# A GpSimd memset in front of every third indirect DMA of the edge scores

## The chip, the cores and the metric

The kernel runs on one core of one Trainium2 chip. The metric is the device time of one execution in microseconds (us), lower is better. PE is the matrix engine, DVE the vector engine, ACT the scalar engine, POOL is GpSimd, SP the engine that issues most of the plain DMAs. A name with a small q (POOLq, SPq) is the sequencer of that engine.

## The reference

Two graph layers are applied to `x` (16 batches, 1024 nodes, 256 features) with one adjacency matrix `adj` (1024 x 1024), most of whose entries are zero. The second layer is the part that matters here:

```python
pre_u = einsum('bud,dk->buk', h_t, W1[:d])
pre_v = einsum('bvd,dk->bvk', h_t, W1[d:])
hidden = relu(pre_u[:, :, None, :] + pre_v[:, None, :, :] + b1)
S = sigmoid(einsum('buvk,ko->buvo', hidden, W2)[..., 0] + b2[0])
a_t = einsum('buv,bud->bvd', S * A_a, h_t)
m_t = einsum('uv,bud->bvd', A_m, h_t) * h_t
z_t = beta1*h_t + beta2*(einsum(a_t, Wa) + ba) + beta3*(einsum(m_t, Wm) + bm)
```

Here `A_a` and `A_m` are both `adj`, and `h_t` is the output of the first layer (a softmax attention over `adj`, all 1024 x 1024 entries). `S` is needed only where `adj` is not zero, because it is multiplied by `A_a`. The kernel therefore computes the scores `S` edge by edge, not for all pairs.

## The kernel before, in words

The first layer and the node projections run batch by batch, on PE above all. For each batch the kernel leaves in DRAM the projections of both ends (`pu_d`, `pw_d`), the features multiplied by `Wa` (`ha_d`) and a partial output (`zb_d`). The batches form three groups of 5, 5 and 6 (`GROUPS`), and a row of `pu_d` or `pw_d` holds one node for all batches of the group.

The edges were sorted before into 21 tiles of 128 lists. A tile has up to 8 places per list, so that there are 135 slots (`SLOTS`), each with 128 edges, one per partition. For each group and each slot `k` the scores go as follows:

- `fetch` (L1201) has POOL issue an indirect DMA that gathers 128 rows of `pw_d` into a buffer `gv` (L1212), and, on the first slot of each tile, one that gathers `gu` out of `pu_d` (L1205). There are five `gv` buffers (`GV`), and slot `k + 3` is fetched when slot `k` is begun (`AHEAD`).
- `compare` (L1235) has DVE combine `gv` with `gu`, in two halves (L1241).
- `sums` (L1248) has ACT add up the columns of each batch into `lg` (L1255); on some slots of the last group DVE does it (L1252). This frees the `gv` buffer.
- `gates` applies the tanh to a part of some 16 slots (L1263), DVE adds 1 (L1282), and the part's scatters are put on the list `late`.
- `scatter` (L1219) has POOL issue an indirect DMA that writes 128 scores of a slot into the dense matrix `sa_d` (L1221). `first`, inside `scores`, takes one or two from `late` after each fetch; what is left after the last slot is issued in one go.

When a group's scores are in `sa_d`, SP loads blocks of it as `sat` (L1325), ACT turns them into `apart` (L1338), DVE multiplies by `adj` (L1343) and PE makes the products with `ha_g` (`gather`, L1356). SP must not load a block before all scatters of the group have landed.

The scores of one group run beside the first layer of the next group's batches, beside the messages (`pm`, L1151), and those of the third group beside the final products (L1356) of the first two. What each engine does next is written out by hand: every step is given a planned time in a `Timetable`, and the steps are emitted in the order of those times. Nothing is reordered at run time; an engine that waits holds up all that stands behind it in its own order.

`upper` (L525) is a 128 x 128 constant in SBUF. PE reads it in four matmuls and weight loads at the start (L563, L768), the last of them 71.6 us into the span, and nothing reads it later.

Of the kernel before, what the change touches and what calls it, by code (L numbers as in the profile page):

```python
# [371 lines left out]
def edge_layers(  # L372
# [36 lines left out]
    nc = tc.nc  # L409
# [115 lines left out]
    upper = const.tile([P, P], F32, name="upper")  # L525
# [383 lines left out]
    st = {}  # L909
# [288 lines left out]
    SA = 7  # L1198
    late = []

    def fetch(g, k):  # L1201
        t, s = SLOTS[k]
        if s == 0:
            gu = st["gu", t] = pools["gath", g].tile([P, SIZE[g] * R], F32, name="gu", bufs=2)
            nc.gpsimd.indirect_dma_start(  # L1205
                out=gu,
                out_offset=None,
                in_=pu_d[g],
                in_offset=bass.IndirectOffsetOnAxis(ap=key_u[:, t : t + 1], axis=0),
            )  # L1210
        gv = st["gv", k] = pools["gath", g].tile([P, SIZE[g] * R], F32, name="gv", bufs=GV)
        nc.gpsimd.indirect_dma_start(  # L1212
            out=gv,
            out_offset=None,
            in_=pw_d[g],
            in_offset=bass.IndirectOffsetOnAxis(ap=idx_v[:, t, s : s + 1], axis=0),
        )

    def scatter(g, lg, i, k):  # L1219
        t, s = SLOTS[k]  # L1220
        dma = nc.gpsimd.indirect_dma_start(  # L1221
            out=sa_d[g],
            out_offset=bass.IndirectOffsetOnAxis(ap=idx_s[:, t, s : s + 1], axis=0),
            in_=lg[:, i, : SIZE[g]],
            in_offset=None,
            bounds_check=N * N - 1,
            oob_is_err=False,
        )
        tc.declare_no_dep(dma.ins, group=f"sa{g}", reason="edges of their own")
        tc.add_to_no_dep_group(f"sa{g}", dma.ins)  # L1230
# [34 lines left out]
    def scores(g, start, end, on_vector):  # L1265

        for k in range(len(SLOTS)):
            time = start + k * (end - start) / len(SLOTS)

            def first(k=k):  # L1270
                for n in range(AHEAD) if k == 0 else ():
                    fetch(g, n)
                if k + AHEAD < len(SLOTS):
                    fetch(g, k + AHEAD)
                for _ in range(min(len(late), 2 if len(late) > PARTS[0] - 4 else 1)):
                    late.pop(0)()

            def last(k=k):
                k0, k1 = place_of(k)
                lg = st["lg", k0]  # L1280
                part = lg[:, : k1 - k0, : SIZE[g]]
                nc.vector.tensor_scalar(part, part, 1.0, None, ALU.add)  # L1282
                late.extend(lambda i=i: scatter(g, lg, i, k0 + i) for i in range(k1 - k0))
# [441 lines left out]
@with_exitstack  # L1725
def tile_graph_layers(ctx: ExitStack, tc: tile.TileContext, *args):
    nc = tc.nc
    I32 = mybir.dt.int32
    hold = ctx.enter_context(tc.tile_pool(name="hold", bufs=1))
    flag = hold.tile([1, 1], I32, name="flag")  # L1730
    edge_layers(tc, *args, flag)
    over = nc.values_load(
        flag[0:1, 0:1],
        min_val=0,
        max_val=1,
        skip_runtime_bounds_check_because="it is a comparison's result",
    )
    with tc.If(over > 0):
        dense_layers(tc, *args)
# [43 lines left out]
```

## Time and profile before

| | us |
|---|---|
| median of 10 runs | 2094.79 |
| lowest and highest of them | 2089.59, 2097.35 |
| the profiled execution | 2090.47 |
| its span, first to last instruction | 2088.8 |

The profiled execution is 1.67 us longer than its span, and 4.32 us below the median of the runs. The granted clock of PE was 0.995 in it. Busy shares of the span were: PE 97%, DVE 75%, ACT 66%, POOL 54%. The 16 DMA engines moved 644.37 MB, 308 GB/s over the span; the queue of the POOL DMAs had 47.6% of the engines' time.

In a line of instruction groups, the figures after the bar are the busy time in us, the mean of one in ns, and the idle time of the engine just before them with what ended most of it. "issue" means that the engine waited for nothing that the profile shows.

### The profile page before, as it was taken

How to read it: one execution, taken by the hardware profiler on the slowest of the kernel's cores; microseconds unless marked ns; L12 is line 12 of the kernel's file. 1: busy time of each engine (PE TensorE's matmuls, PEld its weight loads, DVE VectorE, ACT ScalarE, POOL GpSimd, SP SyncE). 2: the span in 40 equal slices, each digit the busy share in tenths (PEclk: the TensorE clock that was granted, in tenths of full speed). 3: DMA queues.
4: the chain of work that ended last, by engine and by line, in shares of the span. 5: the costliest groups of instructions: out<-in, count | busy, mean ns of one | idle time of the engine just before them, and what ended most of it. 6: DMA issues, size and time to landing. Idle time of an engine off the chain costs nothing.

```text
span 2088.8 us, 28949 instructions
## 1 busy us (share of the span) xinstructions
PE 2025.0 (97%) x8566; PEld 1550.8 (74%) x8566; DVE 1567.1 (75%) x2348; ACT 1374.1 (66%) x4842; POOL 1136.6 (54%) x986
## 2 busy tenths in 40 slices
PE   7999999999999999999999999899999989999998
PEld 5887888777777768576888886456667666778887
DVE  6798886577777677678878885578888878885544
ACT  4212222386867778587888886567888879886654
POOL 2122221257676777668777776666777757673000
PEclk9999999999999999999999999999999999999999
DMA  6597777778888888789999998899999999997873
GB/s 218 209 340 293 290 294 268 245 251 297 282 280 287 271 289 276 263 302 294 304 310 340 311 321 307 316 384 415 386 398 368 411 416 400 391 403 272 282 234 122
DMA packets 248023, 644.37 MB, mean 308 GB/s; under 512 B 37170, under 2 KB 137522, under 8 KB 245810
## 3 DMA queue, kind: packets, MB, share of 16 engines
q0 software_dynamic: 82528, 349.79, 47.6%
q1 hardware_dynamic: 129506, 258.44, 33.6%
q10 hardware_dynamic: 35824, 34.22, 4.7%
q8 instruction: 69, 1.13, 0.2%
q14 instruction: 96, 0.79, 0.1%
HBM read 479.56 MB, written 162.92 MB: 308 GB/s over the span
## 4 chain that ended last, share of the span: by engine, by line
PE 53%; DVE 15%; DMA 14%; ACT 9%; issue 6%; POOL 3%; ACTq 0%; SPq 0%; DVEq 0%; POOLq 0%
PE pv L1053 17%; PE pm L1151 9%; PE pp L1091 7%; DVE gv L1241 6%; DMA gv<-pw_d,idx_v 6%; PE pzg L1356 5%; ACT gv L1255 5%; PE pf L999 4%; DMA sat<-sa_d 3%; PE pea L1119 3%; ACT apart L1338 3%; PE pzh L1356 2%; PE pz L1171 2%; DVE eT L1040 2%; DMA ha_g<-ha_d 2%
## 5 line engine op out<-in xcount | busy, mean ns | idle before, releaser
L1255 ACT ACTIVATE gv<-gv 128x272 f32<-128x272 f32 x2058 | 856.1, 419 | 304.5 <-DVE gv L1241 204.1
L1241 DVE TENSOR_TENSOR gv<-gv,gu 128x680 f32<-128x680 f32 (+1 forms) x810 | 704.4, 906 | 104.5 <-DMA gv<-pw_d,idx_v 100.9
L1212 POOL DMA_INDIRECT gv<-pw_d,idx_v x405 | 486.8, 1202 | 315.3 <-ACT gv L1255 188.7
L1221 POOL DMA_INDIRECT sa_d<-lg,idx_s x405 | 503.1, 1242 | 129.3 <-issue 104.5
L1053 PE MATMUL pv<-feats,eT 128*128 128x257 f32 x2048 | 471.1, 381 | 7.2 <-DVE eT L1040 6.4
L1151 PE MATMUL pm<-adj_sb,xh 128*128 128x512 f32 x1024 | 454.0, 597 | 2.9 <-DVE xh L1067 2.9
L1053 PEld LDWEIGHTS pv<-feats,eT 128*128 128x128 f32 x2048 | 381.3, 190 | 73.2 <-DVE eT L1040 16.8
L1255 ACT ACTIVATION_READ_ACCUMULATOR gv<-gv 128x1 f32 x2058 | 389.1, 189 | 0.0
L1356 PE MATMUL pzg<-ha_g,apart 128*128 128x256 f32 x1536 | 366.7, 381 | 19.6 <-DVE apart L1343 18.9
L1151 PEld LDWEIGHTS pm<-adj_sb,xh 128*128 128x128 f32 x1024 | 194.7, 192 | 223.5 <-issue 220.7
L1356 PEld LDWEIGHTS pzg<-ha_g,apart 128*128 128x128 f32 x1536 | 288.6, 190 | 79.7 <-DVE apart L1343 32.1
L1338 ACT COPY apart<-sat 128x640 f32<-128x640 f32 (+1 forms) x192 | 264.6, 1392 | 80.3 <-PE pzh L1356 45.5
L1343 DVE TENSOR_TENSOR apart<-apart,adj_sb 128x640 f32<-128x640 f32 (+1 forms) x192 | 165.9, 866 | 128.0 <-ACT apart L1338 127.7
L1091 PE MATMUL pp<-wuv,hT 128*128 128x272 f32 x1024 | 249.4, 393 | 4.5 <-ACT end L1105 3.8
L1091 PEld LDWEIGHTS pp<-wuv,hT 128*128 128x128 f32 x1024 | 193.8, 190 | 51.6 <-issue 6.7
L1040 DVE SCALAR_TENSOR_TENSOR eT<-row,col,grown 128x512 f32<-128x512 f32 x256 | 182.8, 744 | 30.7 <-ACT col L986 30.1
L845 POOL DMA_INDIRECT table_d<-rec,at x52 | 57.4, 1104 | 259.6 <-DVE rec L838 157.6
L1084 ACT COPY hT<-ph 128x512 f32<-128x512 f32 x96 | 55.2, 576 | 114.0 <-PE ph L1073 113.9
L1119 PE MATMUL pea<-wa,hT 128*128 128x256 f32 x512 | 121.0, 379 | 0.0
L1171 PE MATMUL pz<-wm,mT 128*128 128x256 f32 x512 | 116.0, 379 | 0.6 <-DVE mT L1162 0.6
L999 PE MATMUL pf<-w1T,xT 128*128 128x257 f32 x512 | 114.9, 381 | 0.5 <-DVE xT L957 0.5
L1356 PE MATMUL pzh<-ha_g,apart 128*128 128x256 f32 x384 | 114.2, 379 | 0.0
(184 smaller groups left out, 1590.3 us busy)
## 6 DMA issues: line engine op xcount, KB each, us to landing
sa_d<-zero SPq DMA_DIRECT2D x128, 512.0 KB, 5.9
sat<-sa_d SPq DMA_DIRECT2D x128, 320.0 KB, 8.8
sat<-sa_d SPq DMA_DIRECT2D x64, 384.0 KB, 5.6
pu_d<-end SPq DMA_DIRECT2D x64, 272.0 KB, 4.3
pw_d<-end SPq DMA_DIRECT2D x64, 272.0 KB, 5.8
ha_d<-ea SPq DMA_DIRECT2D x64, 256.0 KB, 5.1
zb_d<-zb ACTq DMA_DIRECT2D x64, 256.0 KB, 7.8
xh<-in_x_dram SPq DMA_DIRECT2D x15, 1024.0 KB, 12.3
```

Of the source, the lines that this page charges most:

```text
L999: nc.tensor.matmul(pfs[i], lhsT=st["xT"][:, h, c * P : (c + 1) * P], rhs=w1T[:, h, :], start=(h == 0), stop=(h == H - 1),)
L1040: nc.vector.scalar_tensor_tensor(st["eT", b, k, n][:, i, :], st["row"][:, cols], st["col"][:, j : j + 1], grown[:, j, cols], ALU.max, ALU. ...
L1053: nc.tensor.matmul(pv[:, : D + 1], lhsT=st["eT", b, k, j // 4][:, j % 4, i * P : (i + 1) * P], rhs=st["feats", b][:, j, :], start=(j == 0) ...
L1091: nc.tensor.matmul(pp[:, k, :R], lhsT=st["hTi", b, i][:, h, k * P : (k + 1) * P], rhs=wuv[:, side, h, :], start=(h == 0), stop=(h == H - 1),)
L1119: nc.tensor.matmul(pp[:, k, :], lhsT=st["hTi", b, i][:, h, k * P : (k + 1) * P], rhs=wa[:, h, :], start=(h == 0), stop=(h == H - 1),)
L1151: nc.tensor.matmul(pm, lhsT=held[b][:, c, h * P : (h + 1) * P], rhs=adj_sb[:, c, span], start=(c == 0), stop=(c == C - 1),)
L1212: nc.gpsimd.indirect_dma_start(out=gv, out_offset=None, in_=pw_d[g], in_offset=bass.IndirectOffsetOnAxis(ap=idx_v[:, t, s : s + 1], axis=0),)
L1221: dma = nc.gpsimd.indirect_dma_start(out=sa_d[g], out_offset=bass.IndirectOffsetOnAxis(ap=idx_s[:, t, s : s + 1], axis=0), in_=lg[:, i, : ...
L1241: nc.vector.tensor_tensor(mv, mv, mu, op)
L1255: nc.scalar.activation(one[:, j, :], one[:, j, :], AF.Copy, accum_out=lg[:, i, j : j + 1])
L1338: nc.scalar.copy(apart.rearrange("p g v -> p v g"), sat)
L1356: nc.tensor.matmul(st["pzg", g, vc][j // 4][:, j % 4, :], lhsT=apart[:, j, :], rhs=ha, start=(c == 0 and j % 2 == 0), stop=(c == C - 1 and ...
```

## The change

`fetch` and `scatter` call a new function in front of each indirect DMA. It counts the calls, and on every third it has POOL write zeros over `upper`. The count `st["issued"]` runs on through the slots and groups. The indirect DMAs that build the edge lists at the start (L845) don't call it.

```diff
+    def breathe():
+
+        st["issued"] = st.get("issued", 0) + 1
+        if st["issued"] % 3 == 0:
+            nc.gpsimd.memset(upper, 0.0)
+
     def fetch(g, k):
         t, s = SLOTS[k]
         if s == 0:
+            breathe()
             gu = st["gu", t] = pools["gath", g].tile([P, SIZE[g] * R], F32, name="gu", bufs=2)
             nc.gpsimd.indirect_dma_start(
...
+        breathe()
         gv = st["gv", k] = pools["gath", g].tile([P, SIZE[g] * R], F32, name="gv", bufs=GV)
         nc.gpsimd.indirect_dma_start(
...
     def scatter(g, lg, i, k):
         t, s = SLOTS[k]
+        breathe()
         dma = nc.gpsimd.indirect_dma_start(
```

## The prediction

> **What bounds the kernel now.** I read the page's busy shares first, then its chain of waits, then the costliest groups, and after that POOL's own order of instructions. The shares:
>
> ```profile
> PE 2025.0 (97%) x8566; PEld 1550.8 (74%) x8566; DVE 1567.1 (75%) x2348; ACT 1374.1 (66%) x4842; POOL 1136.6 (54%) x986
> ```
>
> PE leaves 64 us of 2088.8 idle. POOL, the engine that the change loads, looks half free. That is the first thing to distrust: the share leaves out what lies between POOL's instructions, and it averages over stages without scores. The chain that ended last and the two large POOL groups:
>
> ```profile
> PE 53%; DVE 15%; DMA 14%; ACT 9%; issue 6%; POOL 3%; ACTq 0%; SPq 0%; DVEq 0%; POOLq 0%
> L1212 POOL DMA_INDIRECT gv<-pw_d,idx_v x405 | 486.8, 1202 | 315.3 <-ACT gv L1255 188.7
> L1221 POOL DMA_INDIRECT sa_d<-lg,idx_s x405 | 503.1, 1242 | 129.3 <-issue 104.5
> ```
>
> Only half of the chain is PE; the rest is the scores' loop (gather, compare, sum) and the loads behind it. The scatters have 104.5 us of idle time before them, over 343 of them, that nothing released: 0.30 us each. POOL's order of instructions shows the same 0.30 us between any two indirect DMAs that stand back to back. So an indirect DMA occupies POOL for its length and 0.30 us more. The scores of group 1 are 135 slots in the 460 us from 856 to 1316, which is 3.41 us a slot. A slot needs one gather (1.202), one scatter (1.242) and 63/405 of a `gu` gather (1.182): 2.63 us, and 2.156 gaps of 0.30 bring it to 3.27. POOL is thus 96% taken there, not 54%. The busy time of POOL in stretches of 50 us (busy, number of instructions, clock, DMA share, GB/s):
>
> ```profile
> 800.00:850.00 50.00, 39.52 (x30) 1.00 0.86 279
> 950.00:1000.00 50.00, 39.64 (x35) 1.00 0.94 303
> 1150.00:1200.00 50.00, 38.88 (x31) 1.00 0.92 312
> 1400.00:1450.00 50.00, 31.67 (x24) 1.00 1.03 413
> ```
>
> With 0.30 us for each instruction, 1.5 us of the first stretch are free, none of the second, 1.8 of the third, 11.1 of the last. Summed over the 29 stretches from 450 to 1900 it is 160 us free of 1450. And the chain itself goes through POOL in places; here is a piece of it (start, length, what):
>
> ```profile
> 1313.99 0.95 POOL gv L1212
> 1314.94 0.30 issue
> 1315.24 1.01 POOL sa_d L1221
> 1316.25 0.30 issue
> 1316.56 0.21 POOL gu L1205
> ```
>
> **The change, part by part.** Nothing is removed, no data moves, and no transfer is added. 63 + 405 + 405 = 873 indirect DMAs call the counter, so 291 memsets are added, all on POOL, spread evenly between 369 and 1904 us. Ten fall in a stretch of 30 DMAs.
>
> *One memset.* The trace has three of this shape at its start, two of them here by form, and the start times of those around:
>
> ```profile
> L537 POOL MEMSET ones<- 128x128 f32 x1 | 0.2, 201 | 0.0
> L526 POOL MEMSET upper<- 128x128 f32 x1 | 0.2, 194 | 0.0
> 1.34 0.19 POOL L526 MEMSET upper<- 128x128 f32 x1
> 1.61 0.29 POOL L527 TENSOR_SCALAR_AFFINE_SELECT upper<-upper 128x128 f32<-128x128 f32 x1
> 1.85 0.20 POOL L537 MEMSET ones<- 128x128 f32 x1
> 1.99 0.95 POOL L659 MEMSET zero<- 128x1024 f32 x1
> ```
>
> So 0.20 us by its length, and by the starts 0.27 (with a successor that reads what it wrote) or 0.14 us (with one that does not). None stands between two indirect DMAs. Bounds for that: nothing, if the memset runs inside the 0.30 us gap that is there anyway; 0.50 us, if it is followed by a gap of its own, 0.20 + 0.30. At the start a plain POOL DMA followed an iota with no such gap (iota 2.90 + 0.37, DMA at 3.23), so I take 0.20. The page "Perfetto Trace Analysis" of the Trainium skill, section "GPSIMD Engine Instruction", says that the reported length of a POOL instruction is unreliable, and that the spacing of starts should be used. By that rule the price is the 0.14 above, and each sum below is seven tenths of what I give.
>
> *What it waits for.* The write over `upper` needs PE's last read of it, at 71.6 us: no wait by 369 us. The memset is emitted in front of the wait of its DMA for a free buffer. Where POOL waits for ACT to free `gv` (188.7 us, 130 gathers) the memset falls into that wait and costs nothing; the cover is gone where the DMA stands under "issue". Behind the memset stand its DMA and all later ones; DVE's compare waits for a gather, and a group's first `sat` load for its last scatter.
>
> *VectorE.* The page "SBUF — State Buffer", section "SBUF: two separate sides", says that GpSimd and VectorE share one pair of ports, held for a whole instruction, against a VectorE operation in a two-port mode, or with two SBUF inputs if the GpSimd one reads. That speaks against the change only for the first kind, since a memset reads nothing. The compares (two SBUF inputs) took 849/860/1079 ns (least, median, longest) beside POOL's DMAs. I charge nothing; were each memset to hold up DVE for its 0.20 us, it would be 58 us of DVE time, spread over all stages.
>
> *What lies on the path.* I counted in the chain the POOL DMAs that follow one another without another engine between, and the gather that ends each such run:
>
> - 451 to 463: 8; 848 to 850: 2; 864 to 869: 4; 894: 1
> - 1035 to 1059: 15; 1188 to 1191: 3; 1303 to 1334: 23; 1372: 1; 1387 to 1388: 2
> - 1436 to 1459: 5; 1585 to 1595: 5; 1847 to 1853: 5
> - the scatters that are left after the last slot, 1876.83 to 1904.85: 18
>
> The last run counts whole although the chain names ACT in the middle of it, since its gaps are the same 0.30 us, and PE does wait at its end:
>
> ```profile
> 1902.60 0.97 POOL L1221 DMA_INDIRECT sa_d<-lg,idx_s  x1 [0.30 <-ACT apart L1338]
> 1903.88 0.97 POOL L1221 DMA_INDIRECT sa_d<-lg,idx_s  x1 [0.30 <-issue]
> 1932.78 1.99 PE L1356 MATMUL pzg<-ha_g,apart 128*128 128x256 f32 x8 [0.56 <-DVE apart L1343]
> 1936.01 1.99 PE L1356 MATMUL pzg<-ha_g,apart 128*128 128x256 f32 x8 [0.38 <-DVE apart L1343]
> ```
>
> After 1936 PE runs without a wait to the end, so what the scatters lose is lost. Together 92 DMAs, some 31 memsets, at 0.20 us 6.1 us (0 to 15.3 by the bounds).
>
> *Off the path.* Elsewhere the free time per stretch covers ten memsets (2.0 us), but for four: 800 (short by 0.5), 950 (2.5), 1100 and 1150 (0.25 each). Those at 800 and 1150 lie beside counted runs; I add the 2.5 of 950, where the chain is now all PE and would turn to the gathers. Three slots of lead, some 10 us, are no cover for that: the gather issued at 463.00 took the chain 12.19 us to land, and DVE waits 100.9 us for gathers in 45 places as it is.
>
> Sum: 6.1 + 2.5 = 8.6 us. On the profiled execution's 2090.47 that gives 2099.1; the median of the runs lies 4.3 higher, and the prediction is 2094.8 + 8.6 = 2103.4 us.
>
> **The rivals.**
>
> *POOL becomes the bound of the scores.* At 0.50 us a memset, a slot of group 1 would need 3.27 + 0.36 = 3.63 us against the 3.41 that it has. The shortfall of all stretches, each against its own free time, sums to 28 us; with 15.3 on the path that is 43 us, 2138. For: the constant gap of 0.30, whose cause the trace does not show. Against: the gapless instructions at the start.
>
> *Covered altogether.* The memset runs in the gap or in waits, price 0 to 0.14: at most 4.3 on the path, 2095 to 2099. For: the sequencer has free time, and the gap is the same whatever came before. That the memset is not executed at all, as a write that nobody reads, I leave out: the copy into `warm` at L503 is never read either, and it is in the trace.
>
> *Faster.* From 1350 to 1850 the DMA share is 1.0, and the chain goes through landings of gathers (5.6% of the span, 117 us) and of `sat` (3.5%, 73 us). POOL's DMAs have a least length of 0.93 to 0.97 us and means of 1.20 and 1.24, so that some 220 us of them are hold-ups. If a pause lets earlier descriptors drain, the next DMA is shorter by what it waited, and the transfers collide less. With a tenth off both landings, 19 us, the net is 8.6 - 19 = -10, 2084. It decides from where landings shorten by over 4.5% of 190 us. Against: POOL issues in bursts because it is behind, and what is issued later lands later.
>
> **How the numbers follow.** Forecast 0.44, POOL as the bound 0.20, covered 0.14, faster 0.22. A difference of 0.2% is 4.2 us, about what a measurement of this kernel can tell from none. The first two end slower, 0.64; covered is the same, 0.14; faster 0.22. The likeliest case alone spans 2099 (0.14 us and nothing off the path) to 2110 (chain at its upper bound). Of the range, 2084 takes in the faster case as priced and 2138 the bound case; I leave out some 0.1 on either side.
>
> **What would show it.** 291 memsets of about 0.20 us on POOL, its busy time up by 58 us; gaps of 0.30 us in front of DMAs after a memset too (none for "covered", two of them for the bound). The last scatter, relative to the last gather, later by 18/3 x 0.20 = 1.2 us. More "DVE gv from DMA gv" than 100.9 us, and PE's idle time up by the sum. It is wrong if the mean lengths of L1212 and L1221 fall by over 0.1 us, or if the chain no longer touches POOL in the places named.

## The result, and the profile after

The changed kernel takes 2098.64 us (median of 14 runs, 2095.37 to 2103.26). The kernel before, measured beside it again, takes 2092.13 us over 50 runs. The ratio is 1.0032 with a 95% interval of 1.0023 to 1.0040: the change costs 6.5 us (4.8 to 8.4). The profiled execution of the changed kernel took 2099.09 us, its span 2097.4 against 2088.8 before.

The added lines move the later lines of the kernel by 7 (the `gu` gather), by 8 (the `gv` gather) and by 9 (from the scatter on). So L1212, L1221, L1241, L1255 and L1356 of before are now L1220, L1230, L1250, L1264 and L1365. From the page of the changed kernel, the shares and the two large POOL groups:

```profile
PE 2028.5 (97%) x8566; PEld 1551.9 (74%) x8566; DVE 1568.0 (75%) x2348; ACT 1374.9 (66%) x4842; POOL 1188.4 (57%) x1277
L1220 POOL DMA_INDIRECT gv<-pw_d,idx_v x405 | 481.6, 1189 | 292.5 <-ACT gv L1264 188.0
L1230 POOL DMA_INDIRECT sa_d<-lg,idx_s x405 | 497.2, 1228 | 114.0 <-issue 93.5
```

POOL has 291 instructions more and is busy for 52 us more. DVE's and ACT's busy times are within 1 us of those before. PE's idle time went from 64 to 69 us, and its busy time from 2025.0 to 2028.5, at a mean granted clock of 0.994 instead of 0.995. The memsets themselves, by form, with busy time and mean ns:

```profile
L1205 POOL MEMSET upper<- 128x128 f32 x291 | 67.8, 233 | 0.0
```

Each takes 0.233 us. What one adds to POOL's order is another matter, and POOL's instructions in order show it (start, length; in brackets the idle time before, and what ended it):

```profile
951.01 1.01 POOL L1230 DMA_INDIRECT sa_d<-lg,idx_s  x1 [0.30 <-issue]
951.99 0.25 POOL L1205 MEMSET upper<- 128x128 f32 x1
952.41 1.24 POOL L1220 DMA_INDIRECT gv<-pw_d,idx_v  x1 [0.16 <-issue]
953.95 1.01 POOL L1230 DMA_INDIRECT sa_d<-lg,idx_s  x1 [0.30 <-issue]
```

The scatter ends at 952.02 and the next gather starts at 952.41: 0.39 us between them, where two DMAs without a memset have 0.30 (953.65 to 953.95). The memset starts just before the DMA ends, and the gap behind it shrinks to 0.16. So it adds 0.09 us, not 0.23: most of it lies in time that POOL lost anyway between two indirect DMAs. This is no single case: at the 231 places of the profile where a memset stands between two indirect DMAs and the second waited for nothing else, the distance is 0.37 to 0.40 us. At most 291 x 0.09 = 26 us were added to POOL's order (a memset that falls into a wait adds nothing), against some 160 us that were free, and yet 6.5 us arrived at the end.

Where they arrived is seen in two long stretches (busy time and number of instructions of PE, PEld, DVE, ACT and POOL, then clock, DMA share, GB/s). The first stretch holds the scores of group 0, the second those of group 1. The kernel before:

```profile
385.00:856.00 471.00, 470.35 (x1937) 349.71 (x1936) 351.36 (x561) 347.81 (x1460) 314.45 (x265) 1.00 0.84 274
856.00:1316.00 460.00, 449.76 (x1965) 352.48 (x1964) 354.63 (x583) 356.96 (x1493) 334.10 (x286) 0.99 0.90 306
```

The changed kernel:

```profile
385.00:856.00 471.00, 471.00 (x1940) 350.57 (x1940) 352.38 (x561) 348.57 (x1464) 330.07 (x354) 1.00 0.85 275
856.00:1316.00 460.00, 445.31 (x1951) 350.44 (x1950) 354.56 (x582) 355.04 (x1480) 345.06 (x376) 0.99 0.89 302
```

In the first PE is as far as before (1940 matmuls against 1937). In the second it does 14 matmuls fewer and has 4.5 us more of idle time. From 1316 to 1876 PE is busy for 534.68 us before and 533.70 after. One such figure is good to some 2 us: the first kernel of the experiments, which costs nothing, has 447.56 in the second stretch. The scores show the place more clearly. From the start of a group's first gather to that of its last, groups 0, 1 and 2 take 487.8, 466.9 and 548.9 us before, and 487.0, 473.6 and 550.6 in the changed kernel: group 1 is 6.7 us longer.

### The profile page after: what moved, and what is told of

Its sections match the earlier page's. It is cut to its first block, busy times and chain, and to the rows that moved or that the text cites. A ratio compares the mean times of both kernels' runs of the same rounds, so it can differ in the third digit from the quotient of the medians.

```text
span 2097.4 us, 29240 instructions
## 1 busy us (share of the span) xinstructions
PE 2028.5 (97%) x8566; PEld 1551.9 (74%) x8566; DVE 1568.0 (75%) x2348; ACT 1374.9 (66%) x4842; POOL 1188.4 (57%) x1277
## 3 DMA queue, kind: packets, MB, share of 16 engines
q0 software_dynamic: 82528, 349.79, 47.6%
## 5 line engine op out<-in xcount | busy, mean ns | idle before, releaser
L1264 ACT ACTIVATE gv<-gv 128x272 f32<-128x272 f32 x2058 | 856.1, 419 | 304.5 <-DVE gv L1250 199.4
L1250 DVE TENSOR_TENSOR gv<-gv,gu 128x680 f32<-128x680 f32 (+1 forms) x810 | 705.1, 906 | 97.3 <-DMA gv<-pw_d,idx_v 96.7
L1220 POOL DMA_INDIRECT gv<-pw_d,idx_v x405 | 481.6, 1189 | 292.5 <-ACT gv L1264 188.0
L1230 POOL DMA_INDIRECT sa_d<-lg,idx_s x405 | 497.2, 1228 | 114.0 <-issue 93.5
L1264 ACT ACTIVATION_READ_ACCUMULATOR gv<-gv 128x1 f32 x2058 | 388.7, 189 | 0.0
L1365 PE MATMUL pzg<-ha_g,apart 128*128 128x256 f32 x1536 | 367.4, 382 | 21.8 <-DVE apart L1352 20.9
L1365 PEld LDWEIGHTS pzg<-ha_g,apart 128*128 128x128 f32 x1536 | 288.0, 190 | 83.8 <-DVE apart L1352 36.6
L845 POOL DMA_INDIRECT table_d<-rec,at x52 | 57.4, 1104 | 259.7 <-DVE rec L838 157.6
L1365 PE MATMUL pzh<-ha_g,apart 128*128 128x256 f32 x384 | 114.2, 379 | 0.0
```

What stands on the lines that cost most here:

```text
L1220: nc.gpsimd.indirect_dma_start(out=gv, out_offset=None, in_=pw_d[g], in_offset=bass.IndirectOffsetOnAxis(ap=idx_v[:, t, s : s + 1], axis=0),)
L1230: dma = nc.gpsimd.indirect_dma_start(out=sa_d[g], out_offset=bass.IndirectOffsetOnAxis(ap=idx_s[:, t, s : s + 1], axis=0), in_=lg[:, i, : ...
L1250: nc.vector.tensor_tensor(mv, mv, mu, op)
L1264: nc.scalar.activation(one[:, j, :], one[:, j, :], AF.Copy, accum_out=lg[:, i, j : j + 1])
L1365: nc.tensor.matmul(st["pzg", g, vc][j // 4][:, j % 4, :], lhsT=apart[:, j, :], rhs=ha, start=(c == 0 and j % 2 == 0), stop=(c == C - 1 and ...
```

## The experiments

Theory A: a memset costs POOL's order a little time, and where POOL is behind, this reaches the end. Against it: that the number of extra instructions counts (B), that the scatters left over at the end are all of it (C), that the cost is spread evenly over the stages (D), that it comes at the end, with the third group (E), that POOL's order matters only at the end (F). Times are against the kernel before, run on the same chip between them. In these diffs a minus line is the changed kernel's unless said otherwise.

**Size, number and the end.** Four kernels on one chip; the kernel before took 2093.23 us there.

```diff
-            nc.gpsimd.memset(upper, 0.0)
+            nc.gpsimd.memset(upper[:, 0:1], 0.0)
```

> The same 291 memsets, each over one column (128x1) in place of 128x128. Theory A, POOL's time: what counts is by how much a memset lengthens POOL's order. In the changed kernel a memset is 0.23 us, starts 0.02 us before the DMA ahead of it ends, and the gap to the next DMA is 0.165 us in place of 0.30, so a back-to-back pair comes 0.10 us later. A memset of 0.11 us (the 128x1 rows at the start: 0.10 to 0.13) then adds next to nothing, 0.00 to 0.02 us, and the time is that of the kernel before, within 2 us. Rival B, the number: each extra instruction between two indirect DMAs disturbs the queue whatever its length; then the time is again 6 us above the kernel before.

Measured 2091.95 us, ratio 0.9998 (0.9987 to 1.0008), that is -2.7 to +1.7 us. Rival B falls: the same 291 places, and no cost. The order of POOL's instructions in this kernel says why:

```profile
1012.73 1.02 POOL L1220 DMA_INDIRECT gv<-pw_d,idx_v  x1 [0.30 <-issue]
1013.75 0.12 POOL L1205 MEMSET upper<- 128x1 f32 x1
1014.06 1.01 POOL L1230 DMA_INDIRECT sa_d<-lg,idx_s  x1 [0.19 <-issue]
```

From the gather's end at 1013.75 to the scatter's start it is 0.31 us, with a memset between; the median of 215 such places is 0.30. A memset of 0.12 us goes into the gap for nothing. It also writes less than the 128 x 128 one, but nothing suggests that the writing is what costs: the compares (median 859 and 860 ns) and the activations of the sums (mean 419 ns) are as long in the changed kernel as before.

```diff
-        st["issued"] = st.get("issued", 0) + 1
-        if st["issued"] % 3 == 0:
-            nc.gpsimd.memset(upper, 0.0)
+        nc.gpsimd.memset(upper, 0.0)
```

> A 128x128 memset in front of every indirect DMA of the scores, 873 in place of 291. Theory A: 92 DMAs on the path by the chain of before x 0.10 us = 9 us, and 8 us of shortfall in the stretches without free time, +17 us; three times the measured 6.5 would be +20. Rival B gives +20 too, so this run tests only that the cost grows with the memsets. Rival C, the scatters left over at the end are all of it: 18 x 0.10 us against 6 x 0.10 us, so at most 2 us more than the changed kernel, +8.

Measured 2109.89 us, ratio 1.0079 (1.0059 to 1.0099), +16.7 us for 873 x 0.09 = 79 us of POOL's order. It grows with the memsets, as A and B both said; C is out, since 873 memsets cost twice what it allowed. Gathers now land too late for DVE more often. The wait (total, times, longest) in the changed kernel, then in this one:

```profile
DVE gv L1250 <- DMA gv<-pw_d,idx_v: 96.7, 47, 11.7
```

```profile
DVE gv L1248 <- DMA gv<-pw_d,idx_v: 143.9, 64, 11.6
```

Four in a row at each third DMA:

```diff
         if st["issued"] % 3 == 0:
-            nc.gpsimd.memset(upper, 0.0)
+            for _ in range(4):
+                nc.gpsimd.memset(upper, 0.0)
```

> Four memsets in a row in front of every third indirect DMA, 1164 in all. Theory A: the first costs 0.10 us, each further one its whole length, 0.23, together 0.79 us; POOL's order grows by 230 us against the 160 us that were free, so POOL becomes the bound: 31 x 0.79 = 24 us on the path plus 85 us of shortfall, +110 us (+60 if the stretches lend each other their free time). Rival B, the number of interrupted pairs: +6 to +26 us (the same 291 places, or four times the 6.5).

Measured 2277.26 us, ratio 1.0893 (1.0867 to 1.0919), +184 us; the expectation was too low by 74. POOL's order shows the mistake:

```profile
1006.80 1.89 POOL L1221 DMA_INDIRECT gv<-pw_d,idx_v  x1 [0.30 <-ACT gv L1265]
1008.69 1.01 POOL L1206 MEMSET upper<- 128x128 f32 x4
1010.22 2.81 POOL L1231 DMA_INDIRECT sa_d<-lg,idx_s  x1 [0.53 <-issue]
```

Four take 1.01 us, and behind four of them the gap is not 0.16 but 0.53 us; why, the trace does not show. From 1008.69 to 1010.22 it is 1.53 us, 1.23 more than without, where I had put 0.79. The median of 173 such places is 1.54 us, but at 24 of them, most in front of a `gu` gather, the gap is about 0.16 here too. So up to 291 x 1.23 = 358 us were added. What took some of it up can be estimated from the two profiles. POOL's idle time beyond these fixed gaps sums to some 160 us before (450 to 1900 us) and to some 30 here (450 to 2080), so that 130 were used up; and a gather takes 1127 ns in place of 1202, which gives 30 back. That leaves 198, near the 184 measured: with POOL as the bound, what is added beyond its free time is paid. PE loses more here than its waits, since its busy time is 2085.1 us against 2025.0, at a mean granted clock of 0.972 against 0.995.

The changed kernel without the memsets in the last flush:

```diff
-        if st["issued"] % 3 == 0:
+        if st["issued"] % 3 == 0 and "tail" not in st:
...
-            times.at(ended, lambda: [late.pop(0)() for _ in range(len(late))])
+            times.at(ended, lambda: (st.update(tail=True), [late.pop(0)() for _ in range(len(late))]))
```

> The changed kernel without the memsets among the scatters that are left after the last slot (5 or 6 of the 291 are gone). Theory A: those lie wholly on the path, 6 x 0.10 = 0.6 us, so +6 us over the kernel before remain. Rival C, the end is what costs: back within 2 us of the kernel before.

Measured 2098.88 us, ratio 1.0028 (1.0014 to 1.0042), +5.7 us, with 5 memsets fewer. The cost remains, so C falls by this too. Its profile repeats what the changed kernel's showed: PE is busy for 442.73 us in the stretch of group 1, and the gathers of groups 0 and 1 take 486.9 and 475.7 us.

**By group, on another chip.** The next four ran on a chip on which the kernel before takes 2117.36 us, with 2102.73 to 2129.09 over 31 runs. `breathe` now takes the group, and the condition is (for group 0, and so on):

```diff
-        if st["issued"] % 3 == 0:
+        if g == 0 and "tail" not in st:
             nc.gpsimd.memset(upper, 0.0)
```

> A memset in front of every indirect DMA of group 0 alone, 291 memsets at 0.09 us back to back (0.39 us between two DMAs in place of 0.30), 26 us of POOL's order. Theory A (POOL's time, passed on where POOL is behind): beside the first group's scores PE ran without idle time and the chain of before went through POOL in ten DMAs only, 10 x 0.09 = 0.9 us: +1 us, within the noise. Rival D, the cost is spread evenly over all stages: a third of the 16.7 us of the run with 873, +5.6.

Ratio 0.9970 (0.9943 to 0.9997), not slower. In this profile PE is busy for all 471.00 us of group 0's stretch; in the other three kernels on this chip, without memsets there, it is 465.10 to 467.90. What the memsets do for PE there was not looked into.

> The same in group 1 alone, where POOL is fullest (3.27 of 3.41 us a slot, with the memsets 3.47): 26 us against 39 us free. Theory A: 33 DMAs of the chain x 0.09 = 3 us, and the shortfalls of the stretches from 950 to 1200 on top of it, 5 us: +8 us. Rival D: +5.6.

Ratio 1.0002 (0.9983 to 1.0021). The +8 us that were expected aren't there.

> The same in group 2 alone, without the scatters left at the end. Theory A: 31 DMAs of the chain x 0.09 = 3 us, hardly any shortfall, since POOL has 71 to 110 us free there: +3 us. Rival D: +5.6.

Ratio 0.9995 (0.9975 to 1.0016).

No group costs anything on this chip, neither as A nor as D said. The stretch of group 1 suggests that something else holds PE up there already (the kernel before left no profile on this chip). This is the kernel with memsets in group 2 alone, thus none in group 1:

```profile
856.00:1316.00 460.00, 434.99 (x1894) 343.14 (x1893) 339.06 (x558) 337.95 (x1407) 322.50 (x273) 0.98 0.88 294
```

PE is busy for 435 us there, not 450, and 71 matmuls fewer are done than before's 1965. POOL's own time an instruction is no longer than before (322.50/273 = 1.18 us against 334.10/286 = 1.17). With 0.30 us for each instruction, POOL has 460 - 322.50 - 273 x 0.30 = 55.6 us free there, against 40.1 before on the other chip. More room for memsets would fit A, but no run tests it. What is slower on this chip was not found, and the groups were tried again elsewhere.

Memsets in the last flush alone, four in front of each scatter (`tail` is set as above):

```diff
-        if st["issued"] % 3 == 0:
-            nc.gpsimd.memset(upper, 0.0)
+        if "tail" in st:
+            for _ in range(4):
+                nc.gpsimd.memset(upper, 0.0)
```

> Four memsets in front of each of the 15 scatters that are issued in one go after the last slot, and no memset elsewhere. The run with four showed 1.24 us for four in a row. Theory A: PE has no time in hand when the last group's blocks arrive (0.56 and 0.38 us of idle time already), so 15 x 1.24 = 19 us arrive whole, +19. Rival: the blocks of group 2 have time in hand, because PE still works on the two other groups; then +0 to +10.

Measured 2132.01 us, ratio 1.0085 (1.0052 to 1.0118), +18 us (11 to 25). The trace shows 13 places of four in that flush, 13 x 1.24 = 16 us. PE's matmuls in order of time show the wait:

```profile
1932.60 0.59 PE L1365 MATMUL pzh<-ha_g,apart 128*128 128x256 f32 x2
1947.30 3.75 PE L1365 MATMUL pzg<-ha_g,apart 128*128 128x256 f32 x8 [14.11 <-issue]
1955.39 1.89 PE L1365 MATMUL pzg<-ha_g,apart 128*128 128x256 f32 x8
```

In the kernel before, the longest wait of PE at this point was 0.56 us. So the last flush is on the path, and what is added there is paid whole. A little comes on top: the eight matmuls behind the wait took 3.75 us, the same eight at 1955.39 took 1.89. The granted clock was 0.82 from 1947 to 1964 us and 1.00 from 1964 to 1981.

**By group again, with their sum beside them.** These ran on a chip where the kernel before takes 2092.54 us. The run with 873 memsets was repeated:

> The run with 873 memsets once more, as the sum for the two parts that run beside it here. Theory A, POOL's time at 0.09 us a memset: +17 us as before (12 to 21). If the device is one where the kernel before takes some 2117 us, as in the runs by group, and the time there lies with transfers: below +8.

Measured 2107.36 us, ratio 1.0075 (1.0060 to 1.0090), +15.7 us.

```diff
+        if g < 2:
             nc.gpsimd.memset(upper, 0.0)
```

> A memset in front of every indirect DMA of groups 0 and 1, none in group 2. Theory A with the place in the path of before: 43 DMAs x 0.09 = 4 us and the shortfalls from 800 to 1200, 5 us: +9 us. Rival E, the loss comes at the end: scores of groups 0 and 1 that come late are made up for before the third group ends, so +0 to +3.

Measured 2107.68 us, ratio 1.0071 (1.0058 to 1.0084), +14.9 us. With `g == 2` in that condition:

> A memset in front of every indirect DMA of group 2, those left over at the end among them. Theory A: 31 x 0.09 + 18 x 0.09 = 4.4 us. Rival E: the remainder of the 17 us, +12 or more.

Measured 2093.21 us, ratio 1.0005 (0.9994 to 1.0015), +1.0 us.

Nearly the whole cost comes from groups 0 and 1, against rival E, and against D, which would have put a third of it, some 5 us, into group 2. The two parts add up: 14.9 + 1.0 against 15.7. Groups 0 and 1 were not run apart on this chip; where their cost arises, the stretches of the kernel with memsets in both show:

```profile
385.00:856.00 471.00, 471.00 (x1941) 350.60 (x1940) 351.27 (x560) 347.51 (x1459) 371.52 (x527) 1.00 0.85 275
856.00:1316.00 460.00, 436.95 (x1914) 346.48 (x1913) 346.61 (x572) 343.31 (x1431) 387.13 (x551) 0.99 0.89 296
```

In group 0's stretch PE has lost nothing. In group 1's it is busy for 12.8 us less than before, nearly the 14.9. From first to last gather, group 0 takes 489.3 us and group 1 482.6, that is 1.5 and 15.7 us more than before. It is thus the scores of group 1 that get longer (some scatters of group 0 are still issued among them). The chain that ended last now runs through POOL for 9% of the span, where it was 3% (the page's line, by engine):

```profile
PE 53%; DVE 12%; DMA 12%; POOL 9%; ACT 8%; issue 5%; POOLq 0%; ACTq 0%; SPq 0%; DVEq 0%
```

That share says what came last, not what it cost: with memsets in group 2 alone it is 7%, for 1.0 us. A piece of the chain in order of time (start, length, what; this view leaves out shorter pieces, some of the memsets among them) has the memsets in it:

```profile
1060.80 0.99 POOL gv L1219
1062.18 1.06 POOL sa_d L1229
1063.23 0.23 POOL upper L1204
1063.62 1.51 POOL gv L1219
...
1082.94 7.40 DMA gv<-pw_d,idx_v
1090.44 0.87 DVE gv L1249
```

POOL works through its list without a wait, the gather that it issues at the end of it lands 7.4 us later, and DVE, with all that stands behind the compare, begins then.

**Taking time out of POOL's order.** The last run goes the other way, from the kernel before. It leaves out every third scatter, so that a third of the edges keep a score of zero:

```diff
     def scatter(g, lg, i, k):
         t, s = SLOTS[k]
+        st["scattered"] = st.get("scattered", 0) + 1
+        if st["scattered"] % 3 == 0:
+            return
         dma = nc.gpsimd.indirect_dma_start(
```

> The kernel before without every third scatter of scores (135 of 405 are left out, so a third of the edges keep a score of zero); no memset. It takes 135 x (1.24 + 0.30) = 208 us out of POOL's order and leaves the gathers, the compares and the sums as they are. Theory A: of the 92 DMAs on the path some 43 are scatters; a third of them, 14, x 1.54 = 22 us would go, less what the next limit (the gathers' landing, PE's own 2025 us) takes back: -8 to -20. Rival F, POOL's order is not on the path except at the end: only the 6 scatters of the last run, 6 x 1.3 = 8 us, of which PE's idle time there gives back 1 to 3 us: -1 to -3.

Measured 2082.46 us, ratio 0.9950 (0.9937 to 0.9963), 10.5 us faster, inside the range of A and far beyond F. Scatters also write to DRAM (4320 of the 82528 packets of POOL's queue are gone), so this is POOL's time and their writes together. The chain by engine, from its page:

```profile
PE 62%; DVE 13%; DMA 12%; ACT 8%; issue 3%; POOL 1%; ACTq 0%; DVEq 0%; SPq 0%; POOLq 0%
```

Its stretch of group 1:

```profile
856.00:1316.00 460.00, 451.32 (x1982) 355.06 (x1981) 359.39 (x590) 360.26 (x1504) 288.50 (x244) 1.00 0.90 309
```

POOL has all but left the chain, and PE does 17 matmuls more than before in this stretch. No kernel here that computes everything is shown to beat the one before; the nearest is that with memsets in group 0 on the second chip (0.9970, at most 0.9997), which was run on that chip alone.

## Why the prediction was right

The forecast was 8.6 us slower; it is 6.5 us, and the mechanism was the one forecast: a little of POOL's time for each memset, paid where POOL is behind. That the size came so near is in part luck. The price of a memset was twice too high and the places where it is paid were counted too few, and the two errors offset each other. Of the 4.8 us between the 2103.4 forecast and the 2098.64 measured, 2.7 lie in the kernel before, which took 2092.13 us beside the changed one and not 2094.79. Step by step:

- **POOL is the near bound of group 1.** Right, and this is what carried the forecast: 3.27 of 3.41 us a slot, read from the gaps and not from the 54% of the page. The runs by group on the third chip place the cost there.
- **The price of one memset, 0.20 us.** Too high by a factor of two: 0.09. I had taken the gap before an indirect DMA as time behind whatever went before. The runs show that a memset runs in it: 0.12 us are free, 0.23 us add 0.09, four in a row add 1.23. The lower bound, "inside the gap", was nearer. By the spacing of starts, as the Trainium skill has it ("Perfetto Trace Analysis", section "GPSIMD Engine Instruction"), it would have been 0.14, nearer than the length of 0.20 but not right either; no row of before has a memset beside an indirect DMA.
- **The count on the path, 92 DMAs, and the 2.5 us of the stretch at 950.** With 0.09 it gives 31 x 0.09 = 2.8 us and 1.2 us for the stretch, 4.0 in all: too low for 6.5 (4.8 to 8.4). The count missed where it lies. 49 of the 92 were in group 2 and in the last flush, and these together cost 1.0 us (interval -1.3 to 3.1) with a memset on every DMA, where the count gave 4.4. Groups 0 and 1 cost 14.9, where it gave 9. The chain of one execution shows what came last in it. That POOL is so full in group 1 that stretches outside this chain get onto it as soon as they are longer would explain the rest; it was not traced place by place.
- **The last flush is paid whole.** Right, by the run with four: +18 us (11 to 25) for 16 added; only 13 of the 18 scatters counted there are issued in the last flush.
- **VectorE is not held up.** Right: compares took 849/859/1080 ns (least, median, longest), 849/860/1079 before.
- **Signs to look for.** POOL's busy time rose by 52 us (58 forecast). The gaps after a memset are 0.16, not 0.30. DVE's waits for gathers fell to 96.7 us in the changed kernel's profile instead of rising; they rose to 143.9 with 873 memsets. PE's idle time rose by 5 us, not by 8.6. From the start of the last gather to the end of the last scatter it is 31.21 us, against 29.27 before: 1.9 more, where 1.2 was forecast, but the kernel with a memset on each DMA of group 2 has 28.37. One profile is too coarse for a cost of 6.5 us. Whether the chain still touches POOL in the places named can't be read from the changed kernel, because its page follows the chain through 8% of the span only; in the kernel without memsets in the last flush, POOL has 4% of it, where it was 3%.

The case "covered" had the right price (0 to 0.14), and most of a memset does run in the gap, but 6.5 us (4.8 to 8.4) is above the 4.3 that it allowed; 2098.64 lies in its 2095 to 2099 only because the kernel before was lower beside it. "POOL becomes the bound" needed 0.50 us a memset; the run with four shows what it looks like. "Faster" has no support: the mean lengths of gathers and scatters fell by 13 and 14 ns in the changed kernel, but were 1189 and 1255 with the small memsets, and no transfer got time back.

Open stays why the second chip is slower with all of these kernels, and why the memsets cost nothing there.

## What to carry to other kernels

For an engine that issues DMAs, add the gaps between its instructions to the busy share, and set the sum against the pace of the stage that it feeds: 54% of the span was 96% of a slot. Of the time added to such an engine a part reaches the end even while the sum over the stages leaves room (6.5 of at most 26 us here, from the fullest stage), and what goes beyond the room arrives (184 of some 358 us, with 160 free before). Whether a small instruction is free depends on the gap that it falls into, which has to be measured at that very place.

## What the runs showed of the hardware

Between two indirect DMAs of POOL lie 0.30 us in which POOL can run something: a memset of 0.12 us left 0.31 us between the DMAs, one of 0.23 us 0.39 us. Four memsets in a row left 1.53 us, with 0.53 us between the last and the DMA. After a wait of 14.11 us PE's next eight matmuls took 3.75 us, where the same eight took 1.89 later, and the granted clock was 0.82 in the 17 us behind that wait. And the same program took 2117 us on one chip and 2092 to 2093 us on two others.
